# A preactivation convolution on one core: the order of PE's sums, of ACT's copies, and who measures which image

## The chip, the cores and the metric

The kernel runs on one core of a Trainium2 chip. The metric is the device time of one execution in microseconds, as the median of several runs. One further execution was taken with the hardware profiler; everything said of engines and waits comes from it. PE is the matmul engine (PEld its weight loads), DVE the vector engine, ACT the scalar engine, POOL the GpSimd engine, SP the engine that issues most of the DMA transfers.

## What is computed

160 images of 128 channels and 32 x 32 pixels, in fp32. Each is normalised over groups of 4 channels, convolved 3 x 3 with quantised weights (image b·5+n of the reshaped batch uses weight set n; the kernel keeps the five sets of 32 images in five stretches), and added to its input.

```python
def _gn(v, G=32, eps=1e-5):
    g = v.reshape(B_, G, C_ // G, H_, W_)
    m = jnp.mean(g, axis=(2, 3, 4), keepdims=True)
    s = jnp.var(g, axis=(2, 3, 4), keepdims=True)
    return ((g - m) / jnp.sqrt(s + eps)).reshape(v.shape)
...
s1 = (beta - alpha) / 3.0            # beta, alpha: max and min of U
v1 = s1 * floor(U / s1)
s2 = s1 / 5.0
v2 = s2 * floor((U - v1) / s2)
w = (v1 + v2).reshape(OUT_CH * N, IN_CH, 3, 3)
x = x + conv(_gn(x), w)              # 3 x 3, padding 1, five groups
```

## The kernel before, in words

An image is one tile of 128 partitions (channels) by 1024. Images come two by two by DMA into a pool of 11 chunks (`xt`). Each image goes through these steps, and the loop in `run` deals with several images at once: in iteration `i` PE convolves image `i` while the other engines work on later ones.

- *Measure* (line 614), for image i+15 from iteration 18 on: a sum (line 241) and a sum of squares (line 248) on ACT, or, for the images that `by_vector` names (line 601), `bn_stats` and a few small instructions on DVE (lines 231 to 235), which come at the end of DVE's iteration. Images are grouped by eight (by two or four at the start), and two tiny matmuls, POOL's power and a few DVE instructions make a group's scales.
- *Split into a high and a low half*, since the matmuls are in fp16 and the sum of two halves keeps the precision. This comes in two kinds. A *combined* image (line 646) gets the differences and sums of neighbouring columns first: POOL lines 673 and 703, DVE lines 685 and 692, for image i+5 in iteration i. Then ACT makes the high half `vh` (line 733, 128 x 2048) of image i+4 and DVE the low half `vl` (line 739, 128 x 2048) of image i+3. For the *other* kind POOL normalises (`z`, line 709; the first image of a group is normalised by ACT, line 635), ACT makes `hi` (line 643, 128 x 1024), and DVE makes `lo` (line 746) and its row combinations (lines 759, 767, 768).
- *Convolve.* The output rows (or columns) are made in pairs, in two banks of PSUM, `even` and `odd`, by a minimal filtering scheme with four products, of which the two inner ones are a sum and a difference product. In a combined image all is done by such products, each for both halves: 24 matmuls. In the other kind the products take only the low half (12 matmuls) and the high half is convolved directly (18 matmuls, line 783): 30 matmuls. All product matmuls are on line 838.
- *The two inner products* are needed in both banks with different signs. `begin(i)` adds the sum product into `even`; ACT copies that bank to `half` (`leave`, line 906); `complete(i)` adds the difference product to the same bank; DVE then makes `odd` = 2 x half - even (line 913). Only after that can `main(i, 0)` and `main(i, 1)` add the outer products to the two banks. So `complete(i)` must wait for the copy, and `main(i, 0)` for line 913.
- *Evict.* In the iteration after, ACT copies both banks into `sum` (line 941), and POOL issues a DMA that adds this tile to the output in HBM (line 962), where the input had been stored before.

There are 4 even banks, 3 odd banks, 2 tiles for `half`, 3 for `sum`. Every engine works through its instructions in the order in which `run` records them; the order is written by hand (`manual_schedule`).

Two orders exist for PE (`conv`, line 862). Without *steady*: begin(i+1), main(i, 0), complete(i+1), main(i, 1), where ACT's `leave(i+1)` is recorded in the middle, before ACT's other work of iteration i. With steady: complete(i+1), begin(i+2), main(i, 0), main(i, 1), where the sums are made two images ahead, and `leave(i+2)` is recorded by `run` in the middle of ACT's iteration. In the kernel before steady starts at image 14 (`FURTHER + 2` is 13).

ACT's order within an iteration from 14 on is: `measure(k, (0,))` (the sum of image i+15), `residual(i - 1)` (two evictions), `leave(i + 2)`, `hi` or `vh` of image i+4, `measure(k, (1,))`. DVE's order is: `vl` or `lo` with its combinations of image i+3, a step or two of quantising the next set's weights (`Later`, in the first 26 or so images of each set but the last), line 913 for image i+1, the scales, lines 685 and 692 for image i+5, a group's statistics if one is ready, and `bn_stats` of image i+15 if DVE measures it.

Through image 14 the statistics also move ahead by one image (`step_of`, around iterations 11 to 13), so that two images are split in one iteration.

Of the kernel before, what the change touches and what calls it, by code (L numbers as in the profile page):

```python
# [36 lines left out]
class Later:  # L37
# [25 lines left out]
    def finish(self):  # L63
        run(self.steps)
# [110 lines left out]
def last_of(steps, last=None):  # L175
    for last in steps:
        pass
    return last


def run(steps):

    while True:
        try:
            next(steps)
        except StopIteration as end:
            return end.value
# [134 lines left out]
def general_path(tc, keep, steps, x, u, out):  # L322
# [8 lines left out]
    with tc.If(far > 0), ExitStack() as ctx:  # L331
# [9 lines left out]
        for n in range(N_SETS):  # L341
            un = one.tile([P, C, TAPS], F32, tag="u", name=f"g_u{n}")
            nc.sync.dma_start(un, uv[n])
            wn = one.tile([P, C, TAPS], F32, tag="w", name=f"g_w{n}")
            k1, k2 = run(steps.quantise(one, un, f"g{n}", F32))
            nc.vector.tensor_scalar_mul(wn, k1, steps.s1)
            nc.vector.scalar_tensor_tensor(wn, k2, steps.s2, wn, ALU.mult, ALU.add)
# [38 lines left out]
class Main:  # L386
# [23 lines left out]

    STAT_LEAD = 15
    FURTHER = 11
    LOAD_LEAD = 18
    CHUNKS = 11
    STEADY = 7
# [174 lines left out]
    def keep_sums(self, n, col):  # L590
        wt = self.wts[n, col]
        run(self.both_sums(
            self.nc.gpsimd, wt[:, self.SUM], wt[:, self.DIFF], *(wt[:, k] for k in range(ROW))
        ))
# [4 lines left out]


    def by_vector(self, i):
        return i in self.BY_VECTOR

    def stats_of(self, k):
        if k not in self.stats:
# [40 lines left out]
    def combined(self, i):  # L646

        if i < self.STEADY or i >= self.imgs:
            return False

        if i < self.FIFTHS:
            return i % 2 == 1
        return i % 5 % 2 == 0 if i < self.THIRDS else i % 4 != 2

    def by_scalar_too(self, i):

# [200 lines left out]

    def steady(self, i):

        return i > self.FURTHER + 2  # L860

    def conv(self, i, on_the_way):

# [118 lines left out]
    def step_of(self, i, ahead):  # L982


        change = self.FURTHER + 4 - ahead
        return [k for k in range(i + ahead + (i > change), i + ahead + 1 + (i >= change)) if k < self.imgs]

    def consumed(self, c):

        return max(i + 2 if self.by_hand(i) else i - 2 - (i > self.FURTHER + 6) for i in range(c * NB, c * NB + NB))  # L990

    def run(self):
# [54 lines left out]
        def measure(stage, *images):  # L1047
            for i in images:
                self.measure(i, (stage,))
# [74 lines left out]
        for i in range(self.imgs):  # L1124
# [53 lines left out]
            if i < self.FIRST:  # L1178

                if i == 0:  # L1180
                    measure(0, 8, 9, 10)
                if i == 1:
                    self.normalise(4)
                    self.high_part(4)
                if i == 2:
                    self.normalise(5)
                    measure(1, 9)
                    self.high_part(5)
                    self.odd_from_even(3)
                    self.low_part(4)  # L1190
                    run(self.combinations(4))
                    measure(0, 11)
                self.residual(j)
            else:

                last = None
                for k in self.step_of(i, 2):
                    if self.combined(k):
                        last = last_of(self.low_combined(k), last)
                    else:  # L1200
                        self.low_part(k)
                        later.take(1)
                        last = last_of(self.combinations(k), last)
                last = later.take(1, last)
                if last:
                    before = self.last_but_one(last)
                    for st in scaled:
                        self.after(st.power(), before)
                    for k in self.step_of(i, 4):
                        self.beside_pairs(k, before)  # L1210
                if i > self.FIRST and self.by_hand(j):
                    self.residual(j)
                for k in by_scalar:
                    self.measure(k, (0,))
                if i > self.FIRST and not self.by_hand(j):
                    self.residual(j)
                    self.accumulate(j)
                if self.steady(i) and i + 2 < self.imgs:
                    self.leave(i + 2)
                for st in ready:  # L1220
                    if not st.late:
                        st.deviations()
                for k in self.step_of(i, 3):
                    if self.combined(k):
                        self.high_combined(k)
                        continue
                    if self.by_scalar_too(k):
                        self.normalise(k)
                    self.high_part(k)
                for k in by_scalar:  # L1230
                    self.measure(k, (1,))
# [31 lines left out]
            if i >= self.FIRST:  # L1263
                measure(0, *by_vector)
# [4 lines left out]
            while loaded * NB < self.imgs and (  # L1269
                loaded * NB < i + self.LOAD_LEAD if loaded < self.CHUNKS  # L1270
                else i >= self.consumed(loaded - self.CHUNKS)
# [55 lines left out]
```

## Time and profile before

| | us |
|---|---|
| median of 3 runs | 971.62 (970.95 to 971.63) |
| the profiled execution | 971.01 |
| its span on the core | 969.3 |
| mean granted PE clock | 0.993 |

| engine | start to start, or mean | what |
|---|---|---|
| ACT | 5.71 us, 4.71 us | one iteration without a break, with `vh` or with `hi` |
| DVE | 2473 ns | `vl` of a combined image |
| DVE | 1646 and 743 ns | lines 685 and 692 of a combined image |
| DVE | 1223, 686, 416 and 416 ns | `lo` and its three combinations |
| DVE | 2 x 679, 209, 154 and 144 ns | an image measured on DVE |
| ACT | 615 and 598 ns | the two evictions of an image |
| ACT | 594 ns | one copy to `half` |

"Busy" in the profile is the time in which at least one instruction of an engine runs. Matmuls are pipelined, so each is recorded as longer than the array is taken by it, and a gap that is shorter than the overlap doesn't show as idle time: for PE the starts must be read too. "Idle before" is time in which an engine stood still just before an instruction, with what ended it. PE's busy share by slices of 24.2 us is 9 tenths or more except in the first slices and in the sixth (121 to 145 us); the granted clock is full but for that time and the start.

### The profile page before, as it was taken

What the parts mean: (1) busy time and instruction counts of PE and PEld (TensorE: products, weight loads), DVE (VectorE), ACT (ScalarE), POOL (GpSimd) and SP (SyncE); (2) the same over time, 40 slices, a digit from 0 to 9 for tenths busy, and PEclk for the clock granted to TensorE, in tenths of its full rate; (3) what the DMA queues carried; (4) which work ended last, traced back from release to release, by engine and by line L of the source; (5) the groups of instructions that cost most, each with busy time, mean ns of one, the idle gap of its engine ahead of it and who ended that gap; (6) DMA issues with size and microseconds to landing.
All of it is one profiled execution on the core that took longest, in us unless ns stands there. A gap on an engine that the chain in (4) does not pass through costs nothing.

```text
span 969.3 us, 13017 instructions
## 1 busy us (share of the span) xinstructions
PE 929.8 (96%) x4432; PEld 435.2 (45%) x4432; DVE 856.0 (88%) x1125; ACT 864.7 (89%) x1320; POOL 447.7 (46%) x481
## 2 busy tenths in 40 slices
PE   2999979999999999999999999999999999999996
PEld 1444434444444444444444444444444444444443
DVE  7988879899798899999999899898989888889973
ACT  5779869999999999999999999999999999998560
POOL 4455433646343453454545444544444354454640
PEclk9999989999999999999999999999999999999999
DMA  9079999999999999999999999999999999756573
GB/s 354 29 272 352 328 359 330 337 311 322 313 331 323 275 268 293 275 293 266 303 240 308 288 275 299 277 276 297 265 270 270 305 258 276 151 87 109 88 109 112
DMA packets 67450, 254.22 MB, mean 262 GB/s; under 512 B 5296, under 2 KB 5296, under 8 KB 67376
## 3 DMA queue, kind: packets, MB, share of 16 engines
q1 hardware_dynamic: 45344, 173.09, 47.5%
q0 software_dynamic: 22032, 80.23, 44.5%
q8 instruction: 36, 0.59, 0.2%
q14 instruction: 38, 0.31, 0.1%
HBM read 89.19 MB, written 164.10 MB: 261 GB/s over the span
## 4 chain that ended last, share of the span: by engine, by line
PE 82%; ACT 9%; DVE 5%; issue 3%; DMA 1%; POOL 0%; ACTq 0%; DVEq 0%; POOLq 0%; SPq 0%
PE even L838 43%; PE odd L838 14%; PE even L783 12%; PE odd L783 12%; ACT vh L733 2%; ACT junk L248 2%; ACT sum L941 1%; ACT junk L241 1%; ACT half L906 1%; DMA xt<-in_x_dram 1%; DVE ext L507 1%; DVE ext L508 1%; ACT z L635 1%; DVE lo L746 1%; ACT hi L643 0%
## 5 line engine op out<-in xcount | busy, mean ns | idle before, releaser
L838 PEld LDWEIGHTS <-wt 128*128 128x128 f16 x1884 | 184.3, 99 | 209.9 <-issue 3.2
L739 DVE SCALAR_TENSOR_TENSOR vl<-v,rstd,vh 128x2048 f16<-128x2048 f32 x94 | 232.5, 2473 | 43.5 <-ACT vh L733 43.3
L838 PE MATMUL even<-vh,across 128*128 128x512 f16 x564 | 211.3, 375 | 3.7 <-ACT half L906 3.7
L838 PE MATMUL even<-vl,across 128*128 128x512 f16 x564 | 211.3, 375 | 1.7 <-DVE vl L739 1.7
L733 ACT ACTIVATE vh<-v,rstd 128x2048 f16<-128x2048 f32 x94 | 190.2, 2023 | 0.0
L783 PEld LDWEIGHTS <-wt 128*128 128x128 f16 x1242 | 122.1, 100 | 145.8 <-issue 8.9
L248 ACT ACTIVATE junk<-xt,mv 128x1024 uint8<-128x1024 f32 x152 | 175.8, 1156 | 0.3
L838 PE MATMUL even<-rows,wt 128*128 128x512 f16 x567 | 174.1, 381 | 1.6 <-ACT half L906 1.5
L241 ACT ACTIVATE junk<-xt 128x1024 uint8<-128x1024 f32 x152 | 160.8, 1058 | 12.9 <-DMA xt<-in_x_dram 9.7
L838 PEld LDWEIGHTS <-across 128*128 128x128 f16 x1128 | 110.4, 98 | 135.8 <-issue 7.8
L783 PE MATMUL even<-hi,wt 128*128 128x496 f16 (+3 forms) x594 | 163.6, 380 | 4.8 <-DVE odd L913 3.8
L709 POOL TENSOR_SCALAR z<-xt,ngm,rstd 128x1024 f32<-128x1024 f32 x49 | 91.6, 1870 | 160.5 <-DVE rows L768 51.3
L783 PE MATMUL odd<-hi,wt 128*128 128x496 f16 (+3 forms) x594 | 161.8, 376 | 0.0
L962 POOL DMA_DIRECT2D out_dram<-sum x153 | 134.1, 876 | 54.6 <-ACT sum L941 47.2
L685 DVE TENSOR_TENSOR v<-xt 128x960 f32<-128x960 f32 x94 | 154.7, 1646 | 1.6 <-POOL v L673 1.6
L673 POOL TENSOR_SCALAR v<-xt,ngm 128x64 f32<-128x64 f32 x94 | 57.9, 616 | 187.4 <-DVE vl L739 80.9
L906 ACT COPY half<-even 128x512 f32<-128x512 f32 x157 | 93.3, 594 | 50.5 <-PE even L838 42.5
L913 DVE SCALAR_TENSOR_TENSOR odd<-half,even 128x512 f32<-128x512 f32 x157 | 108.0, 688 | 22.7 <-PE even L838 19.5
L838 PE MATMUL even<-vh,wt 128*128 128x496 f16 (+1 forms) x282 | 105.6, 375 | 0.0
L838 PE MATMUL even<-vl,wt 128*128 128x496 f16 (+1 forms) x282 | 105.6, 375 | 0.0
L838 PE MATMUL odd<-vl,wt 128*128 128x496 f16 (+1 forms) x282 | 105.6, 374 | 0.0
L838 PE MATMUL odd<-vh,wt 128*128 128x496 f16 (+1 forms) x282 | 105.6, 374 | 0.0
(148 smaller groups left out, 1131.4 us busy)
## 6 DMA issues: line engine op xcount, KB each, us to landing
xt<-in_x_dram SPq DMA_DIRECT2D x78, 1024.0 KB, 8.9
out_dram<-sum POOLq DMA_DIRECT2D x153, 512.0 KB, 8.7
out_dram<-xt SPq DMA_DIRECT2D x76, 1024.0 KB, 13.9
out_dram<-xt SPq DMA_DIRECT2D x7, 512.0 KB, 3.1
u<-in_L_conv_U_dram SPq DMA_DIRECT2D x4, 576.0 KB, 13.6
xt<-in_x_dram SPq DMA_DIRECT2D x4, 512.0 KB, 9.7
range<-in_L_conv_U_dram SPq DMA_DIRECT2D x3, 576.0 KB, 8.0
u<-in_L_conv_U_dram SPq DMA_DIRECT2D x2, 288.0 KB, 3.1
```

What stands on the lines that cost most here:

```text
L241: self.nc.scalar.activation(junk, image, ACTF.Copy, scale=-1.0 / image.shape[1], accum_out=self.mv[:, j, 0:1],)
L248: self.nc.scalar.activation(junk, image, ACTF.Square, bias=self.mv[:, j, 0:1], accum_out=self.mv[:, j, 1:2],)
L673: return self.nc.gpsimd.tensor_scalar(self.view(self.v[i], 0, (512 + W // 2 - 1, 2), (W // 2, H)), self.view(self.image(i), 1, (W - 3, 2), ...
L685: nc.vector.tensor_tensor(self.view(v, 1, (511, 2), (half, H), (1, half - 1)), self.view(x, 1, (1, 2), (W, H), (2, half - 1)), self.view(x ...
L709: ins = nc.gpsimd.tensor_scalar(z, self.image(i), st.ngm[:, j], st.rstd[:, j], ALU.add, ALU.mult)
L733: self.nc.scalar.mul(vh, self.v[i], st.rstd[:, j])
L739: yield self.nc.vector.scalar_tensor_tensor(vl, self.v[i], st.rstd[:, j], self.hi[i], ALU.mult, ALU.subtract)
L783: nc.tensor.matmul(target[a][:, first:end, c0:c1], self.wts[n, col][:, k, :], tile[:, s0 : s0 + 2 * (end - first) - 1 : 2, c0 + dw : c1 + dw],
L838: self.nc.tensor.matmul(out, weights, moving, start=start and j == 0, stop=False, skip_group_check=True)
L906: self.nc.scalar.copy(half, self.eo[i][0])
L913: self.nc.vector.scalar_tensor_tensor(odd, self.half.pop(i), 2.0, even, ALU.mult, ALU.subtract)
L962: added = self.nc.gpsimd.dma_start(self.ov[n, :, b], self.sum.pop(i), accum_op=ALU.add)
```

## The change

Four edits. The order with sums two images ahead starts with image 28 rather than 14. Where it holds, `leave(i + 2)` is recorded before `residual(i - 1)` and `accumulate(i - 1)`, right after the first measurement, rather than after them. Of images 30 to 129, those with i·13 mod 20 below 13 are combined (13 of 20) rather than those with i mod 5 equal to 0, 2 or 4 (12 of 20); before 30 and from 130 on the pattern stays. And every sixteenth image from 48 on (48, 64, 80, 96, 112, 128, 144) is measured on DVE, in addition to the eight images that were.

```diff
     STAT_LEAD = 15
     FURTHER = 11
+    TWO_AHEAD = 28
     LOAD_LEAD = 18
@@ by_vector
-        return i in self.BY_VECTOR
+        return i in self.BY_VECTOR or i > 32 and i % 16 == 0
@@ combined
-        return i % 5 % 2 == 0 if i < self.THIRDS else i % 4 != 2
+        return i * 13 % 20 < 13 if i < self.THIRDS else i % 4 != 2
@@ steady
-        return i > self.FURTHER + 2
+        return i >= self.TWO_AHEAD
@@ run
                 for k in by_scalar:
                     self.measure(k, (0,))
+                if self.steady(i) and i + 2 < self.imgs:
+                    self.leave(i + 2)
                 if i > self.FIRST and not self.by_hand(j):
                     self.residual(j)
                     self.accumulate(j)
-                if self.steady(i) and i + 2 < self.imgs:
-                    self.leave(i + 2)
                 for st in ready:
                     if not st.late:
                         st.deviations()
```

## The prediction

> **What bounds the kernel now.** I read the busy line first, then the busy time by stage, then PE's waits, then the chain, and last the groups that the change multiplies.
>
> The page's busy line:
>
> ```profile
> PE 929.8 (96%) x4432; PEld 435.2 (45%) x4432; DVE 856.0 (88%) x1125; ACT 864.7 (89%) x1320; POOL 447.7 (46%) x481
> ```
>
> Three engines lie within 8% of each other, so what each loses must be read by stage. Columns: stretch, its length, busy us of PE, PEld, DVE, ACT, POOL, clock, DMA share, GB/s. The rows are the start-up of the two-ahead order, most of images 33 to 129, and images 130 to 143:
>
> ```profile
> 120.00:144.00 24.00, 18.24 (x79) 8.09 (x78) 19.19 (x31) 17.26 (x28) 8.24 (x10) 0.86 1.04 361
> ...
> 246.80:795.90 549.10, 549.10 (x2639) 257.67 (x2637) 502.22 (x638) 532.42 (x821) 255.86 (x259) 1.00 1.01 285
> 801.10:880.80 79.70, 77.87 (x370) 36.18 (x369) 68.92 (x70) 75.70 (x115) 37.03 (x39) 1.00 0.77 162
> ```
>
> In the long stretch PE never stops, ACT is idle 16.7 us and DVE 46.9. PE is the bound, the others follow closely. DMA's share is 1.0 there, yet ACT's waits name a transfer only at the start.
>
> PE's own waits (us, times, longest), from 56 to 144 us and then from 144 to 966:
>
> ```profile
> PE even L783 <- DVE odd L913: 3.8, 3, 2.8
> PE even L838 <- ACT half L906: 3.3, 3, 1.8
> PE even L838 <- DVE vl L739: 1.7, 1, 1.7
> ```
>
> ```profile
> PE even L838 <- ACT half L906: 1.8, 3, 0.7
> ```
>
> So after 144 us the copy `half` alone stops PE. This counts only starts after an idle record; since a matmul's record is about 0.16 us longer than its share of the array, I measured starts instead: gaps over 0.2126 us are +0.32 (186.5), +0.36 (334.3), +0.35 (560.7), +1.02 (821.2), +0.90 (843.6), +1.03 (866.2), all at the first difference matmul of an image whose half copy has just ended: 3.98 us. The chain at one of them:
>
> ```profile
> 818.67 0.75 issue
> 819.61 1.03 ACT sum L941 x2
> 820.64 0.48 ACT half L906
> 821.16 2.70 PE even L838 x12
> ```
>
> PE starts when the copy ends, and the copy stood behind the two evictions (`sum`, 1.03 us).
>
> Groups that the change multiplies (count, busy, mean ns, idle before):
>
> ```profile
> L739 DVE SCALAR_TENSOR_TENSOR vl<-v,rstd,vh 128x2048 f16<-128x2048 f32 x94 | 232.5, 2473 | 43.5 <-ACT vh L733 43.3
> L733 ACT ACTIVATE vh<-v,rstd 128x2048 f16<-128x2048 f32 x94 | 190.2, 2023 | 0.0
> ...
> L248 ACT ACTIVATE junk<-xt,mv 128x1024 uint8<-128x1024 f32 x152 | 175.8, 1156 | 0.3
> ```
>
> ```profile
> L231 DVE BATCH_NORM_STATS2 st<-xt 128x6 f32<-128x512 f32 x16 | 10.2, 679 | 0.0
> ```
>
> **What the Trainium skill says.** "TensorE: Matmul & The Clock Gate", section "Wait — 56ns, not 53.3ns?": a warm matmul costs N/2.4 GHz + about 2.5 ns. The trace agrees: six of 512 and 496 columns take 1.27 us. The same page, "What's actually happening": about 3.4 us of idleness halves the clock. The trace shows half clock near 138 to 142 us, after the stall of 3.2 us at 137.7. "Architectural detail" there: ACT and DVE are strict FIFO, so a waiting copy holds what is behind it; the chain above agrees. "ScalarE: Activation LUTs", "What ACT_TABLE_LOAD costs": back-to-back activations overlap by about 93 ns; here two evictions start 0.5 us apart and last 0.6, so I use start-to-start times, not means.
>
> **The change part by part.**
>
> *13 of 20 images combined instead of 12.* Of images 30 to 129, 65 are combined instead of 60. An image of the other kind needs 18 tap matmuls and 12 products, a combined one 24 products: 30 against 24. The instruction order confirms 30 fewer matmuls. In start-to-start times: 24 are two chain pieces of x12 (2.55), 5.1 us; 30 are six of x3 (0.64) and 12 of 0.214, 6.4 us. Saved: 5 x 1.28 = **6.4 us**, all on PE, the bound.
> What it adds: on ACT 5 x 1.0 (5.71 against 4.71 us per image where ACT runs without a break). On DVE 5 x 2.1 (1.65 + 0.74 + 2.48 against 1.22 + 0.69 + 2 x 0.42, less overlaps). POOL is 46% busy. The group starts that ACT normalises (`z`, 1.15 us) fall from 48, 56, 88, 96, 128 to 32, 72, 112.
>
> *Seven images (48 to 144, each 15 images ahead) measured on DVE.* ACT loses 2.35 us each (1.15 + 1.2), DVE gains 2 x 0.68 + 0.21 + 0.15 + 0.14 = 1.87. ACT's neighbours don't wait for DVE's statistics in the built order. In the long stretch, with six of the seven: ACT 532.4 + 5 - 14.1 - 3.5 = 519.8, DVE 502.2 + 10.5 + 11.2 = 523.9, span 549.1 - 6.4 = 542.7. ACT 95.8%, DVE 96.5% full: DVE becomes the second bound, with 19 us to spare.
> Is the slack there locally? I counted matmuls to find each image's pieces. In the two-ahead order `odd` ends 1.2 to 6 us, mostly 3 to 4, before its image's first main matmul. In sums from the timeline DVE's runs of two combined images cost about +1.3 to 2 us over PE, a vector-measured image with a group's statistics 2.6 more: up to some 3.7 us together, just the window. I charge **+0.5**, between 0 and 4.
>
> *Copy ahead of evictions (images 28 on).* `leave` moves past `residual` and `accumulate`: two ACT copies, 1.03 us, and the POOL DMA issue that waits for them; no SP work. The copy can't run before PE's sums for i+2, but where ACT is late PE gets it 1 us earlier. This covers the stalls at 334 and 561 (0.7) and most of the three after 816: ACT needs 3 x 5.71 + 4.71 = 21.8 us per four images, PE without stalls 21.5, the time now is 22.4, and ACT enters less late. I take **-0.7** and **-2.5** (range -1 to -3.6 together). What gets late: evictions of i-1 by up to a wait. Four even and three odd banks, three sums and the 8.7 us accumulate leave over 3 us. `vh` comes after the evictions and can be later by 1 us relative to PE when ACT is ahead; DVE's window for it is still about 3.8 us.
>
> *Two ahead from 28, not 14.* Images 14 to 27 keep the order begin(i+1), main, leave(i+1), complete(i+1), main. The stall at 129 to 138 is untouched: 1.64 (`half`), 2.07 (`vl`), 3.17 (`odd`) and some 2.5 of half clock come from the statistics moving one image further at 11 to 13, which stays; none of PE's work there needs the sums two ahead. The 7.1 us that ACT waits at 144.7 for these sums only moves one copy on. What it costs: the copy's window shrinks from some 3 us to 0.55 (combined i) or 1.7 (other), and `odd` is due 1.9 us earlier (complete(i+1) plus begin(i+2)). ACT's pair of images needs 10.4 of 11.5 us, so bursts decide. Before, double measurements cost +0.58 (91.0) and +2.21 (110.5). From 14 to 27 only image 18 measures two on ACT: +1.1. `odd` of image 22 has 0.32 us to spare and 24 has 1.21: shifted by 1.9 they cost 1.6, less what an earlier stall gives. Against these stands the 0.32 at 186.5. I charge **+1.6**, between -0.5 and +7 (if every image lost the 0.5 us that images 7 to 12 lose: 37.5 us for 34.4 of work).
>
> Sum: -6.4 + 0.5 - 0.7 - 2.5 + 1.6 = **-7.5 us**. The profiled execution took 971.01 (span 969.3 and 1.7 around it): 963.5. The median of the runs is 0.6 above it: **964.1 us**.
>
> **Rivals.**
> - *The early window costs all.* Images 14 to 27 lose 7 us as images 7 to 12 do. For it: ACT is above 95% busy there. Against: six of seven double loads are gone. -6.4 + 0.5 - 3.2 + 7 = -2.1: 969.5. Chance 0.10.
> - *DVE is the bound from 30 to 130.* For it: 96.5% full, 43.3 us of waits for `vh` that may not shrink, bursts as large as the window. Against: these waits have cost PE nothing so far. If it takes back 4 to 5 us: 968.5. Chance 0.14.
> - *Slower: the copy's wait starves DVE.* ACT waits for PE's sums, evicts, then makes `vh`; DVE waits for `vh` and is late with `odd`; PE waits. Place: the 102 images from 28 to 129. It decides once it costs PE more than about 0.074 us per image (the net gain of 7.5 us over 102 images); at 0.11 it costs 11.2 us, 3.7 more than the gain: 975.3. For it: DVE's slack falls by 60%. Against: a 3.8 us window. Chance 0.07.
> - *Nothing lost early, every stall gone:* -6.4 - 4.0: 961.2. Chance 0.09.
>
> **How the numbers follow.** The forecast, PE still the bound with small stalls, has 0.60 and its own range 962 to 967. With 0.2% (1.9 us, what a measurement of this kernel can tell from no change) faster means below 969.7. Faster: 0.60 + 0.09 + 0.13 of the DVE case + 0.05 of the early one = 0.87, lowered to 0.85 for what I have not seen; the same: 0.08; slower: 0.07. The range reaches into the neighbours: 961.5 to 969.
>
> **What would show it.** 30 fewer matmuls, PE 100% from about 230 to 870 us. Right: no starts after `half` over 0.2 us late past 230; images 30 to 129 take 559 to 560 us, not 565.7; ACT near 96% and DVE near 96.5% there; one or two stalls of 1 to 2 us between 150 and 225. Wrong: stalls on `odd` or `vl` past 230, or a half clock in 150 to 225.

## The result, and the profile after

The changed kernel takes 974.3 us (median of 10 runs, 972.89 to 975.67) against 971.09 us of the kernel before (10 runs, 969.9 to 971.66): a ratio of 1.0031 with the 95% interval [1.0023, 1.0040]. It is 3 us slower. The forecast was 7.5 us faster.

In the texts below, A is the two-ahead order from image 28, B the copy ahead of the evictions, C the 13 of 20 combined images, and D the seven images measured on DVE. The quoted expectations number the theories as they came up. Theories 1 to 3 ask which of the four parts takes the time back: 1, that DVE is overfilled between images 33 and 130; 2, that the early images (part A) cost everything; 3, that the copy ahead starves DVE. Theory 4 says: the copy ahead makes `vh` later, DVE has no room to make that good, and PE waits for `vl`. Theory 5 says: the copy ahead makes the evictions later, and PE waits for the banks, or POOL, which issues their DMA, is held up. Theory 6 says: between two copies that wait for PE, only the sum of ACT's work counts, not its order.

The page of the changed kernel: its span, busy time and the chain of waits by engine.

```profile
span 972.8 us, 12884 instructions
...
PE 925.2 (95%) x4402; PEld 432.0 (44%) x4402; DVE 878.9 (90%) x1153; ACT 851.8 (88%) x1290; POOL 459.7 (47%) x488
...
PE 41%; DVE 29%; ACT 17%; issue 8%; DMA 2%; POOL 2%; SPq 0%; ACTq 0%; DVEq 0%; POOLq 0%
```

The 30 matmuls are gone, ACT has 13 us less to do and DVE 23 us more. The chain that ended last ran over PE for 82% of the span before and over DVE for 5%. Now it runs over PE for 41%, over DVE for 29%.

To see where the time went, I counted each image's matmuls in the trace and noted when its first outer product starts (start of the image's `main`). An excess is what one start lies above the usual 0.2126 us after the start before it.

| images | before, us | after, us | forecast change | measured change |
|---|---|---|---|---|
| up to 14 | 137.7 | 138.2 | 0 | +0.5 |
| 14 to 33 | 114.2 | 117.2 | +1.6 | +3.0 |
| 33 to 130 | 549.2 | 549.9 | -6.6 | +0.7 |
| 130 to 159 | 158.2 | 158.0 | -2.5 | -0.2 |

The first row is scatter: nothing is changed there, and over all the profiled kernels it lies between 136.8 and 138.2 us.

The busy time in the last three of these stretches, after, and then in 33 to 130 before (columns: stretch, its length, busy us of PE, PEld, DVE, ACT, POOL, each with its instructions, clock, DMA share, GB/s):

```profile
222.50:255.40 32.90, 31.50 (x149) 14.37 (x148) 27.66 (x33) 29.54 (x45) 15.17 (x16) 1.00 1.04 327
255.40:805.30 549.90, 543.84 (x2607) 254.52 (x2606) 523.81 (x667) 520.69 (x791) 271.56 (x267) 1.00 1.00 282
805.30:963.40 158.10, 156.43 (x744) 72.80 (x743) 133.37 (x133) 118.52 (x169) 77.86 (x74) 1.00 0.68 134
```

```profile
251.90:801.10 549.20, 549.20 (x2640) 257.90 (x2639) 500.82 (x638) 532.52 (x818) 258.02 (x261) 1.00 1.01 285
```

In the long stretch PE has 33 matmuls fewer, about 7 us by 0.2126 us each, and yet the stretch is 0.7 us longer: PE, which had no idle record there, now has 6 us of them. The clock is full, and the DMA rate has not risen. PE's waits (us, times, longest), after, from 144 to 248 us, from 248 to 801 us and from 801 to 970 us:

```profile
PE even L839 <- ACT half L907: 2.1, 3, 1.1
```

```profile
PE even L839 <- DVE vl L740: 4.4, 7, 1.7
PE even L839 <- DVE rows L768: 0.8, 1, 0.8
PE even L839 <- ACT half L907: 0.7, 1, 0.7
```

```profile
PE even L839 <- ACT half L907: 1.7, 3, 0.6
```

Before, there was none of these but three waits for `half` after 801 us (1.8 us in all). By starts, the excess in 33 to 130 is 5.94 us for `vl` in nine places, 1.00 for `half`, 0.97 for `rows` and 0.37 for `odd`: 8.3 us, against 0.3 before. That is the whole gain and a little more. The chain of waits at the longest of them, a wait for the `vl` of image 119 (start, us, what):

```profile
723.14 1.91 POOL rstd L286
725.06 0.02 issue
725.08 0.37 DVE rstd L307
725.45 0.00 issue
725.46 1.99 DVE v L686
727.44 0.66 DVE v L693
728.11 0.53 DVE tt L144
728.63 2.27 DVE vl L740
730.91 0.04 issue
730.95 2.50 PE even L839 x11
```

This `vl` doesn't wait for `vh`: DVE comes to it late, from a row of its own work, and PE stands until `vl` ends. But the row starts with a late `vh`. Followed further back, the chain reaches image 114:

```profile
694.07 1.91 ACT vh L734
696.00 1.67 DVE vl L740
```

There DVE had stood for 1.95 us until `vh` ended. In the 35 us from that start to PE's at 730.95 it is idle only once for longer than 0.1 us, the 0.96 us for POOL's power. What `vh` is late at the head of such a row is not made good in it. The groups that the forecast multiplied:

```profile
L740 DVE SCALAR_TENSOR_TENSOR vl<-v,rstd,vh 128x2048 f16<-128x2048 f32 x99 | 241.9, 2443 | 31.9 <-ACT vh L734 31.5
...
L734 ACT ACTIVATE vh<-v,rstd 128x2048 f16<-128x2048 f32 x99 | 200.3, 2023 | 1.4 <-DVE v L693 1.4
```

DVE's idle time ahead of `vl` fell from 43.3 to 31.5 us over the kernel. DVE's waits from 248 to 801 us, before and after:

```profile
DVE vl L739 <- ACT vh L733: 21.3, 20, 2.5
DVE rstd L307 <- POOL rstd L286: 9.6, 10, 1.0
DVE odd L913 <- PE even L838: 8.8, 9, 1.4
```

```profile
DVE rstd L307 <- POOL rstd L286: 11.5, 12, 1.0
DVE vl L740 <- ACT vh L734: 10.0, 8, 2.9
```

DVE was idle 48 us in this stretch before and is idle 26 us now. The wait for POOL's power comes with every group of images, about 1 us each, before and after. So 11.5 of the 26 us were not free for other work in this order, and the times that DVE waited for PE, a sign that it was ahead, are gone.

### The profile page after: what moved, and what is told of

It reads as the page before. It is cut to its first block, busy times and chain, and to the rows that moved or that the text cites. A ratio compares the mean times of both kernels' runs of the same rounds, so it can differ in the third digit from the quotient of the medians.

```text
span 972.8 us, 12884 instructions
## 1 busy us (share of the span) xinstructions
PE 925.2 (95%) x4402; PEld 432.0 (44%) x4402; DVE 878.9 (90%) x1153; ACT 851.8 (88%) x1290; POOL 459.7 (47%) x488
## 4 chain that ended last, share of the span: by engine, by line
PE 41%; DVE 29%; ACT 17%; issue 8%; DMA 2%; POOL 2%; SPq 0%; ACTq 0%; DVEq 0%; POOLq 0%
PE even L839 21%; PE odd L839 7%; PE even L784 7%; DVE v L686 6%; PE odd L784 6%; DVE vl L740 5%; ACT vh L734 5%; ACT sum L942 4%; ACT junk L248 3%; DVE odd L914 3%; DVE lo L747 2%; DVE v L693 2%; ACT junk L241 2%; POOL rstd L286 2%; DMA xt<-in_x_dram 2%
## 5 line engine op out<-in xcount | busy, mean ns | idle before, releaser
L839 PEld LDWEIGHTS <-wt 128*128 128x128 f16 x1884 | 184.1, 99 | 212.8 <-issue 5.3
L740 DVE SCALAR_TENSOR_TENSOR vl<-v,rstd,vh 128x2048 f16<-128x2048 f32 x99 | 241.9, 2443 | 31.9 <-ACT vh L734 31.5
L839 PE MATMUL even<-vl,across 128*128 128x496 f16 (+1 forms) x594 | 222.5, 375 | 6.2 <-DVE vl L740 6.1
L839 PE MATMUL even<-vh,across 128*128 128x496 f16 (+1 forms) x594 | 222.6, 375 | 5.3 <-ACT half L907 5.3
L734 ACT ACTIVATE vh<-v,rstd 128x2048 f16<-128x2048 f32 x99 | 200.3, 2023 | 1.4 <-DVE v L693 1.4
L784 PEld LDWEIGHTS <-wt 128*128 128x128 f16 x1152 | 113.3, 100 | 135.2 <-issue 9.0
L686 DVE TENSOR_TENSOR v<-xt 128x960 f32<-128x960 f32 x99 | 169.6, 1714 | 0.0
L674 POOL TENSOR_SCALAR v<-xt,ngm 128x64 f32<-128x64 f32 x99 | 68.1, 688 | 209.7 <-DVE vl L740 74.9
L839 PE MATMUL even<-rows,wt 128*128 128x512 f16 x522 | 160.1, 380 | 3.4 <-ACT half L907 2.5
L784 PE MATMUL even<-hi,wt 128*128 128x512 f16 (+1 forms) x549 | 151.6, 380 | 4.8 <-DVE odd L914 3.8
L784 PE MATMUL odd<-hi,wt 128*128 128x512 f16 (+1 forms) x549 | 149.8, 376 | 0.0
```

The source lines that it names most:

```text
L674: return self.nc.gpsimd.tensor_scalar(self.view(self.v[i], 0, (512 + W // 2 - 1, 2), (W // 2, H)), self.view(self.image(i), 1, (W - 3, 2), ...
L686: nc.vector.tensor_tensor(self.view(v, 1, (511, 2), (half, H), (1, half - 1)), self.view(x, 1, (1, 2), (W, H), (2, half - 1)), self.view(x ...
L734: self.nc.scalar.mul(vh, self.v[i], st.rstd[:, j])
L740: yield self.nc.vector.scalar_tensor_tensor(vl, self.v[i], st.rstd[:, j], self.hi[i], ALU.mult, ALU.subtract)
L784: nc.tensor.matmul(target[a][:, first:end, c0:c1], self.wts[n, col][:, k, :], tile[:, s0 : s0 + 2 * (end - first) - 1 : 2, c0 + dw : c1 + dw],
L839: self.nc.tensor.matmul(out, weights, moving, start=start and j == 0, stop=False, skip_group_check=True)
```

## The experiments

Ratios are to the kernel before, with 95% intervals. "33 to 130" is the time from the first outer product of image 33 to that of image 130, 549.2 us in the kernel before.

| run | parts | median, us (before) | ratio | 33 to 130, us |
|---|---|---|---|---|
| a_only | A | 971.98 (971.04) | 1.0008 [1.0001, 1.0014] | 549.2 |
| b_only | B | 971.59 (971.04) | 1.0009 [1.0000, 1.0017] | 549.2 |
| c_only | C | 966.55 (971.04) | 0.9957 [0.9944, 0.9971] | 543.8 |
| d_only | D | 971.21 (971.04) | 1.0002 [0.9994, 1.0011] | 549.2 |
| no_a | BCD | 973.08 (970.97) | 1.0024 [1.0011, 1.0036] | 549.9 |
| no_b | ACD | 970.22 (970.97) | 0.9994 [0.9985, 1.0002] | 545.9 |
| no_c | ABD | 972.40 (970.97) | 1.0013 [1.0007, 1.0020] | 549.7 |
| no_d | ABC | 969.86 (970.97) | 0.9988 [0.9979, 0.9996] | 545.6 |
| bc | BC | 969.23 (971.47) | 0.9971 [0.9959, 0.9983] | 545.5 |
| cd | CD | 969.12 (971.47) | 0.9976 [0.9967, 0.9986] | 545.9 |
| after_vh_first | ABCD, evictions last | 979.85 (971.47) | 1.0087 [1.0072, 1.0103] | 550.3 |
| c_vh_first | BC, evictions last | 976.88 (971.47) | 1.0059 [1.0045, 1.0072] | 547.8 |
| no_b_vh_late | ACD, `vh` late | 970.58 (970.80) | 0.9999 [0.9991, 1.0007] | 547.6 |
| c_tail | C, 3 more on DVE | 964.76 (970.80) | 0.9941 [0.9927, 0.9954] | 543.8 |
| c_plus | C, 7 more on DVE | 962.27 (970.80) | 0.9908 [0.9895, 0.9922] | 541.9 |

### Each part alone

*a_only*, the two-ahead order from image 28:

```diff
+    TWO_AHEAD = 28
-        return i > self.FURTHER + 2
+        return i >= self.TWO_AHEAD
```

> Only the start of the two-ahead order moves from image 14 to 28. Theory 1 (DVE is overfilled between images 33 and 130 and takes back the matmul saving): this part costs what its traces show before image 33, +2 to +3 us, and nothing later. Theory 2 (the early window is the whole loss): +4 us or more, since the other parts would then gain together. Theory 3 (the copy ahead of the evictions starves DVE): nothing to +1 us.

Measured: +0.9 us, little more than can be told. In images 14 to 33 the excess for `half` rises from 0.11 to 0.86 us, one wait at 171 us. The stretch as a whole is 114.2 us as before, because PE's late starts at the low clock near 138 us happened to cost 0.7 us less in this execution, as they also did in d_only, without A.

*b_only*, the copy ahead of the evictions:

```diff
+                if self.steady(i) and i + 2 < self.imgs:
+                    self.leave(i + 2)
                 if i > self.FIRST and not self.by_hand(j):
                     self.residual(j)
                     self.accumulate(j)
-                if self.steady(i) and i + 2 < self.imgs:
-                    self.leave(i + 2)
```

> Only the copy to half moves ahead of the evictions, from image 14 on. Theory 1: -1 to 0 us (the small stalls at 186, 334 and 561 us go; those at 821, 843 and 866 stayed in the changed kernel and stay here). Theory 3 (the copy's wait starves DVE): +2 us or more, with DVE's idle time before vl longer than 43 us and PE waiting for vl.

Measured: +0.5 us, at the edge of what can be told. PE's waits from 800 to 970 us in this run:

```profile
PE even L838 <- ACT half L906: 1.7, 3, 0.6
```

The three waits that this part was to remove stand there, three times, nearly as long as before (1.8, longest 0.7). The two small ones between 33 and 130 stay as well (0.28 us by starts, 0.29 before).

*c_only*, 13 of 20 combined:

```diff
-        return i % 5 % 2 == 0 if i < self.THIRDS else i % 4 != 2
+        return i * 13 % 20 < 13 if i < self.THIRDS else i % 4 != 2
```

> Only the pattern of combined images, 65 of 100 instead of 60. Theory 1: the 30 matmuls save 6.4 us and DVE, 10 us fuller, gives back a part: -5 to -2 us, PE waits for vl short. Theory 2 and 3: the full -6 us. If the pattern by itself (two runs of two) is to blame and not DVE's sum: 0 or slower.

Measured: -4.5 us, the only part that gains. Of the 6.4 us of matmuls most arrives; PE's waits from 250 to 800 us show what doesn't:

```profile
PE even L838 <- ACT half L906: 1.4, 2, 0.8
```

By starts 2.15 us in four places, and 0.91 us more in 14 to 33. ACT is 98.0% busy in 33 to 130 here, DVE 93.9%, and PE has none of the waits for `vl` that theory 1 expected. So C alone makes ACT the tight engine, not DVE.

*d_only*, seven images measured on DVE:

```diff
-        return i in self.BY_VECTOR
+        return i in self.BY_VECTOR or i > 32 and i % 16 == 0
```

> Only the seven images that DVE measures. ACT 16 us emptier, DVE 13 us fuller, no matmul saved. Theory 1: -0.5 to +2 us, since DVE goes to about 94% and its bursts of 1.9 us plus a group's statistics meet a window of some 3 us. Theory 2 and 3: -1 to 0 us.

Measured: no change that can be told. PE is the bound either way. The four parts alone add up to +0.9 + 0.5 - 4.5 + 0.2 = -2.9 us; together they make +3.2. Six microseconds come from parts meeting each other. Neither theory 1 nor theory 3 holds for a part alone.

### The change without one part

Each undoes one of the diffs above in the changed kernel, and nothing else.

```diff
-        return i >= self.TWO_AHEAD
+        return i > self.FURTHER + 2
```

> The changed kernel with the two-ahead order from image 14 again. Theory 1: it stays slower than or near the kernel before, 0 to +1.5 us, because the stalls on vl between 248 and 801 us (8 us) remain. Theory 2: -4 us or better. Theory 3: as the changed kernel, +3 us.

```diff
-                if self.steady(i) and i + 2 < self.imgs:
-                    self.leave(i + 2)
                 if i > self.FIRST and not self.by_hand(j):
                     self.residual(j)
                     self.accumulate(j)
+                if self.steady(i) and i + 2 < self.imgs:
+                    self.leave(i + 2)
```

> The changed kernel with the copy behind the evictions again. Theory 1: within 1 us of the changed kernel, +2 to +4. Theory 3: the stalls on vl go, -4 us or better.

```diff
-        return i * 13 % 20 < 13 if i < self.THIRDS else i % 4 != 2
+        return i % 5 % 2 == 0 if i < self.THIRDS else i % 4 != 2
```

> The changed kernel with 60 of 100 images combined. Theory 1: the stalls on vl nearly go with 10 us of DVE's work, but so does the saving of 6.4 us: +1 to +3 us against before. Theory 2: as the changed kernel or slower, +3 to +9.

```diff
-        return i in self.BY_VECTOR or i > 32 and i % 16 == 0
+        return i in self.BY_VECTOR
```

> The changed kernel without the seven images on DVE. Theory 1: most of the stalls on vl go while the matmul saving stays, -3 to 0 us against before. If ACT (then near 98% full) is needed emptier: stalls on half in their place and +2 us or more. Theory 3: +3 us.

Measured: without A the kernel is 1.0024 of before, hardly better than with it (1.0031, and the intervals overlap); the long stretch is the same 549.9 us, so theory 2 falls. Without B or without D it is 0.9994 and 0.9988: leaving out either one brings the long stretch down by 4 us. PE's waits from 250 to 800 us without B:

```profile
PE even L839 <- ACT half L907: 1.3, 2, 0.7
PE even L839 <- DVE vl L740: 0.6, 1, 0.6
PE even L839 <- DVE rows L768: 0.3, 1, 0.3
```

With the same instructions on every engine, and DVE 95.9% busy in 33 to 130 (95.3% in the changed kernel), the wait for `vl` is 0.6 us in one place, against 4.4 in seven (by starts 1.3 against 5.9 us). What B does is to move a copy, so the place of the copy makes these waits, given D's and C's load on DVE. Without C (549.7 us) there is no wait for `vl` at all.

How a moved copy does it shows in `vh`. The copy waits for PE's sums; the evictions, which were done before that wait, now come after it and ahead of `vh`. I measured when `vh` ends, from the first outer product of the image four before. The least value in a kernel is 2.7 us without B and 3.7 us with it, 1.0 us later. DVE's wait for `vh` from 250 to 800 us, without B:

```profile
DVE vl L740 <- ACT vh L734: 5.9, 5, 2.0
```

With B it is the 10.0 us shown above. At the wait for image 119's `vl` the row of DVE's work is the same without B, but its head comes earlier against PE: PE waits 0.78 us by starts instead of 1.85. DVE waits for POOL the same 11.5 us with B and without, so POOL is not the way. How long before its need `vl` is ready falls accordingly, as a mean over 33 to 130: 3.67 us before, 2.71 with B alone, 2.62 with C alone, 3.32 with D alone, 1.92 without B, and 1.38 in the changed kernel. At the worst image it is 2 us too late there.

### Two pairs

*cd* and *bc* have two of the four diffs each.

```diff
     # cd
-        return i in self.BY_VECTOR
+        return i in self.BY_VECTOR or i > 32 and i % 16 == 0
-        return i % 5 % 2 == 0 if i < self.THIRDS else i % 4 != 2
+        return i * 13 % 20 < 13 if i < self.THIRDS else i % 4 != 2
```

> The pattern and the seven images on DVE, without the other two parts. Theory 1 with DVE's fill alone to blame: DVE 95 to 96% full as in the changed kernel, waits for vl of 4 us or more, 970 us or more. Theory 4 (the fill does harm only with the early copy): waits for vl of 1 to 2 us, 967 to 969 us.

```diff
     # bc
-        return i % 5 % 2 == 0 if i < self.THIRDS else i % 4 != 2
+        return i * 13 % 20 < 13 if i < self.THIRDS else i % 4 != 2
+                if self.steady(i) and i + 2 < self.imgs:
+                    self.leave(i + 2)
                 if i > self.FIRST and not self.by_hand(j):
                     self.residual(j)
                     self.accumulate(j)
-                if self.steady(i) and i + 2 < self.imgs:
-                    self.leave(i + 2)
```

> The pattern and the early copy, without the other two parts. Theory 4: the pattern fills DVE to 94% and the early copy takes 1 us of its window: 967 to 969.5 us, with waits for vl where the pattern alone has none. Theory 5 and any in which the two simply add (-4.5 and +0.6 us): 967.1.

Measured: 0.9976 for cd and 0.9971 for bc, where C alone is 0.9957. In the long stretch B takes back 1.7 us of C's gain and D 2.1 (545.5 and 545.9 against 543.8), and the excess for `vl` is 1.69 us with B and 1.30 with D, about as theory 4 has it. Both together take back 6 (549.9 in no_a). D was to relieve ACT, but the waits for `half` stay (2.07 us in cd, 2.15 in c_only): images 48, 64 and so on are not where ACT falls behind.

### `vh` ahead of the evictions

If lateness of `vh` is the cause, `vh` may be put ahead of the evictions too, with the copy still first. *after_vh_first* does so in the changed kernel, *c_vh_first* in the kernel with B and C.

```diff
-                if i > self.FIRST and not self.by_hand(j):
+                late = self.steady(i) and i > self.FIRST and not self.by_hand(j)
+                if i > self.FIRST and not self.by_hand(j) and not late:
                     self.residual(j)
                     self.accumulate(j)
...
                     self.high_part(k)
+                if late:
+                    self.residual(j)
+                    self.accumulate(j)
```

> The changed kernel, but from image 28 on ACT makes the high half right after the copy and evicts after it. Theory 4 (the copy ahead makes vh 1 us later against PE, since it waits for PE's sums with the evictions and vh behind it, and a DVE that is 95% full can't make this good): vh's least distance after its iteration's first main matmul falls from 3.66 us to 2.7 or less, PE's waits for vl fall from 6 us to 1 or 2, and the time to about that of the changed kernel without the early copy, 970 us. Theory 5 (the later evictions do the harm, through the banks or through POOL, whose DMA issue waits for them ahead of v and z): the evictions come later still, so no better than the changed kernel, 973 to 976 us.

> The kernel before with the new pattern of combined images, the copy ahead, and the high half ahead of the evictions. Theory 4: the 2.2 us of PE's waits for half between 33 and 130 that the pattern alone has go, and no waits for vl come: 964 to 966 us. Theory 5: slower than the pattern alone (966.6), 968 or more.

Measured: 1.0087 and 1.0059, slower than anything else. PE's waits from 250 to 800 us, in the changed kernel with `vh` first:

```profile
PE even L839 <- ACT sum L942: 5.7, 8, 1.6
```

The waits for `vl` are gone (by starts 0.12 us instead of 5.94), as theory 4 says, but both times miss what it expected. `begin` now waits for a bank that has not been evicted: 7.39 us by starts in 33 to 130 and 6.95 after 130. While PE stands for a bank DVE goes on, so these two runs can't tell how much of the cure is `vh`'s. The banks had less room than I thought when I wrote that four and three banks leave over 3 us. These waits do not occur in the changed kernel itself, so the banks do not explain its time; they set a limit to the repair.

### `vh` late without touching the copy

*no_b_vh_late* leaves copy and evictions where the kernel before had them (parts A, C, D) and puts the second measurement, 1.2 us of ACT, ahead of `vh`.

```diff
+                if self.steady(i):
+                    for k in by_scalar:
+                        self.measure(k, (1,))
                 for k in self.step_of(i, 3):
...
                     self.high_part(k)
-                for k in by_scalar:
-                    self.measure(k, (1,))
+                if not self.steady(i):
+                    for k in by_scalar:
+                        self.measure(k, (1,))
```

> The changed kernel with the copy behind the evictions again, but with ACT's sum of squares (1.2 us) moved ahead of the high half from image 28 on: vh is late, the copy and the evictions stay as before. Theory 4 (B's harm is the lateness of vh): vh's least distance rises from 2.69 to about 3.85 us, PE's waits for vl from 1.3 to 6 us or more, and the time from 970.2 to 973 to 976 us, without any later eviction. Theory 5 (the later evictions do it): no change, 970 to 971 us.

Measured: 970.58 us, ratio 0.9999. The time is what theory 5 expected; the waits are theory 4's:

```profile
PE even L839 <- DVE vl L740: 3.7, 5, 1.7
PE even L839 <- ACT half L907: 0.3, 2, 0.2
PE even L839 <- DVE rows L768: 0.3, 1, 0.3
```

By starts the excess for `vl` rises from 1.26 to 4.49 us, and at image 119 from 0.78 to 1.85, as with B. A late `vh` makes PE wait for `vl`, with the copy and the evictions unmoved: that is shown. In 33 to 130 it costs 1.7 us (547.6 against 545.9 without B). The rest is offset, since the waits for `half` fall at once, from 2.12 to 0.66 us in this stretch and from 2.35 to 1.43 us after 130, where `vl` holds nothing up.

For the second fall the order itself is the reason: it makes ACT's iteration shorter. Two copies that follow each other without idle time of ACT, in no_b and then in no_b_vh_late (start, us, what):

```profile
835.95 0.59 ACT L907 COPY half<-even 128x512 f32<-128x512 f32 x1
841.68 0.58 ACT L907 COPY half<-even 128x512 f32<-128x512 f32 x1
```

```profile
837.15 0.61 ACT L907 COPY half<-even 128x512 f32<-128x512 f32 x1
842.70 0.62 ACT L907 COPY half<-even 128x512 f32<-128x512 f32 x1
```

They lie 5.73 us apart, and 5.55 with the sum of squares ahead of `vh`. ACT's busy time in 33 to 130 falls from 520.0 to 514.9 us. So this edit does two things, and its total time can't be set against theory 4's. That PE's waits for `vl` also give ACT time to catch up is likely in 33 to 130, but not shown.

### Taking ACT work away where the copy is late

Why did B not remove the waits after 816? Theory 6: with the copies waiting on PE, ACT's work from one copy to the next is the same set of instructions in either order, so where ACT is the late one, the copies come at ACT's pace. Then only less work between the copies can help. *c_tail* has C, and images 147, 151 and 155 are measured on DVE: 2.35 us less for ACT at each of the three waits after 816. *c_plus* has images 45, 65, 85 and 125 on DVE as well, whose measurements lie ahead of the waits for `half` in c_only. Neither has A, B or D.

```diff
-        return i in self.BY_VECTOR
+        return i in self.BY_VECTOR or i in (147, 151, 155)                      # c_tail
+        return i in self.BY_VECTOR or i in (45, 65, 85, 125, 147, 151, 155)     # c_plus
```

> The pattern alone, with images 147, 151 and 155 measured on DVE: each lies between the two copies of ACT before the stalls near 817, 840 and 862 us. Theory 6 (between one copy that waits for PE and the next, the order of ACT's work is of no consequence, only its sum is; that is why the copy ahead left these stalls at 2.1 us): taking 2.35 us of work out of each stretch ends these stalls, -2 us against the pattern alone, 964 to 965 us, since DVE is only 87% full there. If DVE can't hold it: waits for vl in their place and 966 to 968.

> As the last, with 45, 65, 85 and 125 measured on DVE too, which lie before the stalls on half near 244, 356, 468 and 693 us. Theory 6: another -1.5 to -2 us, 962 to 963.5 us. Theory 1 (DVE's bursts between 33 and 130 have no room left): waits for vl come in their place, 964 to 967 us.

Measured: 0.9941 and 0.9908. In c_tail no wait for `half` is left after 800 us, and 130 to 159 takes 156.2 us instead of 158.2. In c_plus only 0.18 us is left in 33 to 130, in one place. It is the best version, 962.3 us, better than both kernels, and as theory 6 expected. Its page:

```profile
span 961.5 us, 12955 instructions
...
PE 922.8 (96%) x4402; PEld 431.9 (45%) x4402; DVE 879.3 (91%) x1153; ACT 851.9 (89%) x1290; POOL 460.8 (48%) x488
```

Busy time and counts are those of the changed kernel, engine by engine: 879.3 against 878.9 us on DVE, 851.9 against 851.8 on ACT, the same 4402 matmuls. The span is 11.3 us shorter. Over the whole kernel the two do the same work; the images that DVE measures are others, and A and B are absent. In 33 to 130 only three of the seven are measured, so DVE works 515.8 us there against 523.8; its share is the same, 95.2% against 95.3%. DVE's waits in it from 250 to 800 us:

```profile
DVE rstd L307 <- POOL rstd L286: 11.5, 12, 1.0
DVE vl L739 <- ACT vh L733: 10.0, 10, 2.1
```

These are the totals of the changed kernel, with no wait of PE beside them. So a DVE that is 95% busy doesn't by itself cost the time.

## Why the prediction was wrong

*The matmuls.* Right: -6.4 us was forecast for 30 matmuls. c_plus, where PE waits for next to nothing, takes 541.9 us in 33 to 130, 7.3 us less than before. The cut at the two starts takes in 33 matmuls fewer (7.0 us), and 0.3 us were waits.

*"Copy ahead of evictions", -0.7 and -2.5.* This step failed first, in its sign. The stalls were read correctly off the chain (the copy behind two evictions), but the remedy was not one: -3.2 us were forecast, alone it brings +0.5, and the three late waits stay at 2.1 us by starts (2.3 before). I had put ACT's 21.8 us of work against PE's 21.5 in four images and drawn from it that ACT "enters less late"; but by that sum ACT is the slower of the two, and then the order between its copies can't help. c_tail, which takes work away, ends these waits. My list of gaps was wrong as well: the six numbers that I called gaps over 0.2126 us were distances from start to start. Over 0.2126 they are 0.11, 0.15, 0.14, 0.81, 0.69 and 0.82 us, so 2.7 us could be had at most, not 4.0. The stalls at 91 to 138 us are distances too, each 0.21 us too large.

*"DVE's window for it is still about 3.8 us".* This is the step that made the kernel slower. I gave `vh` a lateness of up to 1 us, and that is what was measured. The window was mis-sized. In the kernel before, `vl` is ready 3.8 us before its need in the middle of the images from 33 to 130 (median), but only 0.99 us at the tightest, image 119: the very place of the longest wait after. And the usual 3.8 us were already wanted by the combined images in a row and by the measurements on DVE, which I had myself put at "up to some 3.7 us together, just the window". I took the two steps each as if alone, and charged +0.5. PE's waits for DVE's tiles (`vl`, `rows` and `odd`) came to 7.3 us there, where there had been none. The sign of being wrong that I had named, stalls on `odd` or `vl` past 230 us, is what the trace shows. I had cited the Trainium skill's section "Architectural detail" of the page "TensorE: Matmul & The Clock Gate", on ACT and DVE as strict FIFO, for the stalls that B was to remove. The same sentence holds for the copy that B moves. `vh` stood behind it before as well, but now the two evictions, 1.03 us, stand between the copy and `vh`, and the trace agrees with its 1.0 us.

*"19 us to spare".* DVE's busy time in the long stretch was forecast at 523.9 us and is 523.8. But idle time was taken for slack, and 11.5 us of what is left are waits for POOL's power.

*"Two ahead from 28, not 14", +1.6.* The size is near by luck: A alone costs 0.9 us, and the stretch lost 3.0. Alone it brings one wait for `half`, at image 20; the waits for `odd` at images 22 and 24 that I had priced don't come. In images 14 to 33 the excess for `half` is 0.86 with A, 0.91 with C and 2.58 where both are present, 0.8 more than the two add up to. The extra lies at the copies of images 32 and 33, just after images 29 to 31, three combined in a row with the new pattern. The timeline at the last of these waits in the changed kernel:

```profile
245.21 0.57 ACT L907 COPY half<-even 128x512 f32<-128x512 f32 x1
245.68 0.63 ACT L942 COPY sum<-even 128x512 f32<-128x512 f32 x1
245.83 0.38 PE L839 MATMUL even<-vh,across 128*128 128x512 f16 x1 [1.11 <-ACT half L907]
```

The copy already stands ahead of the evictions, and is late all the same. The 2.58 us are the same without B and without D. That A and C meet here is read from these traces; the pair alone was not tried. A reading on the way was wrong as well: the half clock that I put at 138 to 142 us, after the stall, holds from 135.6 to 142.4 us. It begins 0.7 us after PE went idle, with two shorter stalls before it, so this trace doesn't show how much idle time it takes.

*The rivals.* "The copy's wait starves DVE" was given 0.07. Its mechanism is what happened (`vh` late, DVE late, PE waits), at 8 us over the images from 33 to 130, just beyond its threshold of 7.5 in all. It named `odd` as the late tile, and PE waited for `vl`. It also took B to do this alone, and B needs C for it, and grows with D. Alone it costs 0.5 us, beside C 2.2 us (bc against c_only, each set against its own runs of the kernel before), beside A, C and D some 4. "DVE is the bound" had the load nearly right (96.5% against 95.3%) and the reason wrong: without B, at the same DVE load, `vl` holds PE for 1.3 us by starts instead of 5.9.

What stays open: whether relieving DVE of the wait for POOL's power would have saved the changed kernel was not tried, nor B and D without the others, nor the copy ahead in c_plus.

## What to carry to other kernels

An engine's busy share is no budget: the changed kernel and the best version have the same busy time on every engine and differ by 11.3 us of span. Count for each wait how early its input is ready, at the tightest place and not on average, and subtract from that one number everything that the edits take from it together. Where an engine works in strict order between two points at which it waits for another, moving an instruction forward made what it passed late and left the pace as it was; taking work out of that very interval helped. Put relief at the images where the wait is seen, not at even distances.

## What the runs showed of the hardware that was not expected

Line 685 (686 after), a difference of an image's columns with both inputs in SBUF, was priced at its mean of 1646 ns, but it has two durations. Of the 58 from images 33 to 130 before, 12 ran with no POOL computation beside them, 11 of these beside a DMA issue of POOL, and took 1.15 us. The other 46 started while a POOL computation ran, its difference of columns (line 703), and took 1.56 to 2.01, on average 1.79. One of each kind, from the timelines before and after (start, us, what):

```profile
303.99 0.89 POOL L962 DMA_DIRECT2D out_dram<-sum  x1 [2.64 <-ACT sum L941]
304.02 1.15 DVE L685 TENSOR_TENSOR v<-xt 128x960 f32<-128x960 f32 x1
```

```profile
725.39 1.03 POOL L704 TENSOR_TENSOR v<-xt 128x512 f32<-128x512 f32 x1
725.46 1.99 DVE L686 TENSOR_TENSOR v<-xt 128x960 f32<-128x960 f32 x1
```

In the second, DVE ends 1.03 us after POOL does. All 46 before and all 60 such after end 1.01 to 1.06 us after POOL's computation, however much of it was left, as if DVE got nothing done while it ran. The Trainium skill, page "SBUF — State Buffer", says in the section "Who interferes with whom" that a DVE instruction with two inputs in SBUF contends with a GpSimd instruction that reads SBUF, and in the section "Summary: rules for kernel authors" that the second of such a pair to issue is fully blocked until the first finishes. The traces agree, for POOL first; DVE was never first here. After the change 60 of 62 had a POOL computation beside them, and the mean in this stretch rose from 1655 to 1778 ns. In c_plus it is 1764, so this is not what sets the two apart; whether POOL's columns could be made at another time was not tried.
